# A graph layer that gathers some of its rows by picking columns: VectorE's 32 picks a run in three groups instead of two

## The chip, the cores and the metric

The kernel runs on one core of one Trainium2 chip. The metric is the time of one execution on the device in microseconds; lower is better. The core's engines are TensorE (PE in the profile, with its weight loads as PEld), VectorE (DVE), ScalarE (ACT), GpSimd (POOL) and SyncE (SP). Each has its own instruction queue, which runs in order. What a queue executes itself, such as loading registers or waiting, is shown as DVEq, ACTq, POOLq, SPq.

## The reference

A message-passing layer over a graph of N = 12,500 nodes with 128 features and E = 412,500 edges, sorted by their target node, with a residual connection and a layer norm.

```python
f0 = x0 @ W1_0e / sqrt(32);  f1 = einsum('nui,uw->nwi', x1, W1_1o) / sqrt(32)   # per node
e0, e1 = feat0[edge_src], feat1[edge_src]                 # a row of 128 gathered per edge
h = gelu(edge_scalar_attr @ W_mlp1 / sqrt(8));  h = gelu(h @ W_mlp2 / sqrt(64)) # per edge
w00, w01, w10, w11 = h @ Wp_00, h @ Wp_01, h @ Wp_10, h @ Wp_11
out0_a = w00 * e0 * ea0
out0_b = w11 * sum(e1 * ea1[:, None, :], -1) / sqrt(3)
out1_a = (w01 * e0)[:, :, None] * ea1[:, None, :]
out1_b = w10[:, :, None] * e1 * ea0[:, :, None]
n0, n1 = segment_sum(mid0, edge_dst), segment_sum(mid1, edge_dst)               # over edges
y = cos(pi/8) * self + sin(pi/8) * (n @ W2 / sqrt(64))    # scalar part and vector part
result = layernorm(x + y)
```

## The kernel before, in words

**Runs and groups.** The edges are cut into 806 runs `s` of 512, a run into four columns `q` of 128 edges. Four runs make a group `c` (CH = 4; k = s mod 4 is the place in the group). One loop over the runs issues everything, and the order in it is the order on the engines: PE, ACT, DVE and SP are scheduled by hand, so each queue executes its instructions as the loop writes them.

**Ahead of the loop.** The node rows are turned (`xT`, nodes along the free dimension, kept in on-chip memory for all 12,500 nodes) and multiplied by `wf` into the table of features. The first 18 runs ("raw" runs) gather rows of x and make their features themselves (`turn_rows`, `features`, L555 to L569); the later ones gather from the table.

**The rows of a run** land in a buffer `G` with four columns; 19 such buffers are in use (LEAD). A column is filled in one of four ways:
- by GpSimd's indirect DMA of 128 rows (`gather`, L210), which is the ordinary way;
- in every 14th run one column by 128 small DMAs on SyncE's queue (`aid`, L193 and L197);
- in every fourth run (18, 22, ...) column 2 by VectorE: it copies 128 columns of `xT`, one for each edge, into a tile `gt` (`pick`, L178). Then TensorE multiplies `gt` by `wf` (`picked_rows`, L186) and ScalarE copies the product into `G` (L187), two runs ahead of use;
- in the same manner column 1 in about every fifth run by ScalarE (L180).

The address of a picked column is a number from the input. So ahead of a group of picks, its engine's queue loads that many numbers from on-chip memory into registers (`pick_nodes`, L167, `TENSOR_LOAD`), and each copy reads its address from a register. VectorE picks 32 columns a run for one target; ScalarE picks 24 or 28 a run, 128 in five runs. Picks are spread over the runs ahead of their target. `COL_TURN` says in which run they begin and at which place k in a group their product stands: k = 0 for VectorE's picks, k = 1 for ScalarE's. So ScalarE's targets stand 4 or 8 runs apart.

**VectorE in a run.** `messages` makes the products of weights `w` (PSUM) and rows `G` in three instructions, 0 (L592, 128x256), 1 and 2 (L596, 128x384 each), into `M`. Between them stand the picks:

```python
messages(s, 0)
messages(s, 1)
pick_nodes(DVE, s, 0, 2)     # load 16 addresses
pick(DVE, P // 16)           # 8 copies
messages(s, 2)
pick_nodes(DVE, s, 1, 2)     # load 16 addresses
pick(DVE, P)                 # the 24 that are left
```

At k = 2 an addition of the last group's sums follows (`add`, L636); at k = 3 the selection for the next group (`select`: `oh` L577, then `own` L585). About every eighth group ends with a normalisation (`moments`, `normalise`), in which VectorE takes statistics (`bst`, L665) of what TensorE and ScalarE made of the sums (`y`, L656 and L661). Afterwards parts of the accumulator are cleared, one in a run (L406).

**TensorE in a run:** weights of coming runs (L550), sums of the run before (L621, L623, which need `M` and `own`), at k = 0 also the turning of edge attributes (L508), then `picked_rows` if one is due, then at k = 2 and 3 the two layers of the small network (`mlp1` L517, `mlp2` L532). ScalarE evaluates their gelu (L521, L537). The turning, the picked product and both layers take their PSUM tiles from one pool, "h", of two buffers.

Of the kernel before, what the change touches and what calls it, by code (L numbers as in the profile page):

```python
# [8 lines left out]
F32 = mybir.dt.float32  # L9
# [3 lines left out]
AF = mybir.ActivationFunctionType  # L13
OP = mybir.AluOpType
PE = mybir.EngineType.PE
ACT = mybir.EngineType.Activation
DVE = mybir.EngineType.DVE
# [4 lines left out]
P = 128  # L22
# [4 lines left out]
SB = P * Q  # L27
J = 8
CH = 4
# [18 lines left out]
AID_FROM = 36  # L48
AID_LEAD = 16
STEPS = 12  # L50
COLS = {DVE: 4, ACT: 5}
COL_Q = {DVE: Q - 2, ACT: Q - 3}
COL_TURN = {DVE: (8, 0), ACT: (16, 1)}
LNB = 2


# [1 line left out]
def gnn_kernel(ctx: ExitStack, tc: tile.TileContext, x, src, dst, ea4, ea8, w1_0, w1_1, wm1, wm2,  # L58
# [8 lines left out]
    nc = tc.nc  # L67
    N, F = x.shape
    E = src.shape[0]
    NS = -(-E // SB)  # L70
# [7 lines left out]
    raw_runs = min(RAW, NS)  # L78

    cst = ctx.enter_context(tc.tile_pool(name="cst", bufs=1))  # L80
    wk = ctx.enter_context(tc.tile_pool(name="wk", bufs=2))
# [3 lines left out]
    def sub(ap, offset, dims):  # L85
        return bass.AP(tensor=ap.tensor, offset=ap.offset + offset, ap=dims)


    x_at, _ = nc.bump_sbuf(4 * N)
    xT = nc.alloc_sbuf_tensor_at("xT", [P, N], F32, offset=x_at).ap()  # L90
    x_bytes = xT.bitcast(U8)
    x_bytes = bass.AP(tensor=x_bytes.tensor, offset=x_bytes.offset - x_at, ap=[[4 * N, P], [1, x_at + 4 * N]])
# [18 lines left out]
    G, GT, Y = {}, {}, {}  # L111
    aided = range(AID_FROM, NS - 1, AID)

    picked = {}
    for e, per in COLS.items():
        picked[e], (t, k) = [], COL_TURN[e]
        while True:
            at = t + per + 1
            at += (k - at) % CH
            if at + 2 >= NS - 1:  # L120
                break
            picked[e].append((t, at, at + 2))
            t += per
    pick_of = {(e, s): i for e, g in picked.items() for i, (_, _, s) in enumerate(g)}
    assert AID_FROM >= raw_runs and AID_LEAD < LEAD and P % ROWS == 0 and STEPS <= AID
    assert all(raw_runs <= g[0][2] and 0 < len(g) <= 2 * P for g in picked.values())
    assert 0 < len(aided) <= P

    aid_at = cst.tile([len(aided), P], I32)
    pick_rows = {}  # L130

    def aid_load():


        nc.sync.dma_start(aid_at, sub(src, AID_FROM * SB + (Q - 1) * P, [[AID * SB, len(aided)], [1, P]]))
        for e, g in picked.items():
            cycle = CH // math.gcd(CH, COLS[e])
            for h in range(0, len(g), P):
                part = g[h:h + P]
                rows = cst.tile([len(part), P], I32, name=f"pick{len(pick_rows)}")  # L140
                for i in range(min(cycle, len(part))):
                    n = len(part[i::cycle])
                    nc.sync.dma_start(rows[i::cycle], sub(src, part[i][2] * SB + COL_Q[e] * P,
                                                          [[cycle * COLS[e] * SB, n], [1, P]]))
                pick_tiles.append(rows)
                for i in range(len(part)):
                    pick_rows[e, h + i] = rows[i:i + 1]
# [7 lines left out]

    picking = {e: [] for e in picked}

    def pick_nodes(e, s, part=0, parts=1):

        per = COLS[e]  # L160
        i, t = divmod(s - COL_TURN[e][0], per)
        if not 0 <= i < len(picked[e]):
            return
        if t == 0 and part == 0:
            GT[e, i] = wk.tile([P, P], F32, name=f"gt{list(picked).index(e)}", bufs=3)
        r0, r1 = (n * (P // 4) // (per * parts) * 4 for n in (t * parts + part, t * parts + part + 1))
        _, r = nc.values_load_multi_w_load_instructions(  # L167
            pick_rows[e, i][:, r0:r1], engines=[e], min_val=x_at, max_val=x_at + 4 * (N - 1),
            skip_runtime_bounds_check_because="addresses of columns")
        for k in range(r1 - r0):  # L170
            at = r[k].with_bounds(guaranteed_mod_val=0, out_of_modulus=4)
            picking[e].append((GT[e, i][:, r0 + k:r0 + k + 1], x_bytes[:, bass.ds(at, 4)].bitcast(F32)))

    def pick(e, n):

        for to, col in picking[e][:n]:
            if e == DVE:
                nc.vector.tensor_copy(to, col)  # L178
            else:
                nc.scalar.activation(to, col, AF.Copy)  # L180
        del picking[e][:n]

    def picked_rows(e, i):

        pt = ps.tile([P, P], F32, name="h")
        nc.tensor.matmul(pt, GT.pop((e, i)), wf, start=True, stop=True)  # L186
        nc.scalar.activation(G[picked[e][i][2]][:, COL_Q[e], :], pt, AF.Copy)  # L187

    def aid(s, t):

# [397 lines left out]
    def messages(s, part):  # L588
        w, g = WP[s], G[s]
        if part == 0:  # L590
            M[s] = wk.tile([P, Q, 2, P], F32, name="M", bufs=3)
            nc.vector.tensor_tensor(M[s][:, :, :, :MUL], w[:, :, :2 * MUL].rearrange("p q (a u) -> p q a u", a=2),  # L592
                                    g[:, :, None, :MUL].to_broadcast([P, Q, 2, MUL]), op=OP.mult)
            return
        j = part - 1
        nc.vector.tensor_tensor(M[s][:, :, j, MUL:].rearrange("p q (i u) -> p q i u", i=3),  # L596
                                w[:, :, None, (2 + j) * MUL:(3 + j) * MUL].to_broadcast([P, Q, 3, MUL]),
                                g[:, :, MUL:].rearrange("p q (i u) -> p q i u", i=3), op=OP.mult)
# [221 lines left out]
    with tc.manual_schedule(engines={PE, ACT, DVE, SP}):  # L820
# [34 lines left out]
        if aided:  # L855
            aid_load()
# [9 lines left out]
        features(0)  # L866
        A["now"] = A["next"]
        clearing = []
        pick_nodes(ACT, 0)
        for s in range(NCH * CH + CH):  # L870
            c, k = divmod(s, CH)
            if s + LEAD - 1 < NS:
                gather(s + LEAD - 1)
            if k == 3 and c + EDGES_AHEAD < NCH:
                load_edges(c + EDGES_AHEAD)
            if s % P == P // 2 - 16 and (s // P + 1) * P < NS:
                load_raws(s // P + 1)
            if s % P == P // 2 and (s // P + 1) * P < NS:
                load_indices(s // P + 1)
            if s % ET == 8 and s - 8 + ET < NS:  # L880
                load_attributes(s // ET + 1)
            for t in range(P // ROWS):
                a = s + AID_LEAD - t * STEPS // (P // ROWS)
                if a in aided:
                    aid(a, t)
            end = c == NCH - 1
            if k % 2 == 0:
                pick(ACT, len(picking[ACT]) // 2)
            if k % 2 == 0 and s + 2 < NS:
                weights(s + 2, range(Q // 2))  # L890
            if k % 2 == 1 and s + 1 < NS:
                weights(s + 1, range(Q // 2, Q))
            if 0 < s <= NS:
                segments(s - 1)
            if k == 0 and c < NCH:
                places(c)
            if k == 0 and c + 2 < NCH:
                radial(c + 2)
            if s % ET == 21 and s - 21 + ET < NS:
                turn_attributes(s // ET + 1)  # L900
            for e in picked:
                if (e, s + 2) in pick_of:
                    picked_rows(e, pick_of[e, s + 2])
            if k > 1 and c + 2 < NCH:
                pick(ACT, P)
                (mlp1 if k == 2 else mlp2)(c + 2)
                if k == 3 and c + 3 == NCH:
                    nc.scalar.activation(spent, ones, AF.Sqrt)
            pick(ACT, P)
            pick_nodes(ACT, s + 1)  # L910
            if s + 1 < raw_runs:
                turn_rows(s + 1)
            if s < NS:
                messages(s, 0)
                messages(s, 1)
                pick_nodes(DVE, s, 0, 2)
                pick(DVE, P // 16)
                messages(s, 2)
                pick_nodes(DVE, s, 1, 2)
                pick(DVE, P)  # L920
            if s + 1 < raw_runs:
                features(s + 1)
            if k == (1 if end else 2) and 0 < c <= NCH:
                add(c - 1)
            if k == (1 if end else 3) and 0 < c <= NCH:
                norm(due.get(c - 1, []), last=c == NCH)
                clearing += [(c, a) for a in range(4)] if c - 1 in due and c < NCH else []
            elif clearing:
                clear_sums(clearing.pop(0)[1])
            if k == 3 and c + 1 < NCH:  # L930
                select(c + 1)
            if s == 1:
                addresses()
                find_first()
                new_sums()
                clearing = [(0, a) for a in range(4)]
            if s == NS - 8:
                count_odd()
# [31 lines left out]
```

## Time and profile before

| | |
|---|---|
| median of 3 runs | 3773.7 us |
| lowest, highest | 3766.81, 3779.11 us |
| profiled execution | 3772.84 us |
| its span, first to last instruction | 3771.0 us |
| granted TensorE clock, mean | 0.914 |
| table gathers by GpSimd (L210) | 2743 |
| picked columns, VectorE (L178) | 25216, in 788 runs |
| picked columns, ScalarE (L180) | 19968 |

Engine times in the profile are busy times of one execution. "Idle before, releaser" is the time that the engine stood still right ahead of such an instruction, and what ended it; "issue" means that the engine waited for nothing that the profile shows, only for its queue to hand it the instruction. The timeline's rows give the start in us from the start of the span, the duration in us, then engine, line and operation, and a count where several like ones are merged. Durations of neighbours overlap a little, so what an instruction takes of the engine's time is read from the starts.

### The profile page before, as it was taken

What the parts mean: (1) busy time and instruction counts of PE and PEld (TensorE: products, weight loads), DVE (VectorE), ACT (ScalarE), POOL (GpSimd) and SP (SyncE); (2) the same over time, 40 slices, a digit from 0 to 9 for tenths busy, and PEclk for the clock granted to TensorE, in tenths of its full rate; (3) what the DMA queues carried; (4) which work ended last, traced back from release to release, by engine and by line L of the source; (5) the groups of instructions that cost most, each with busy time, mean ns of one, the idle gap of its engine ahead of it and who ended that gap; (6) DMA issues with size and microseconds to landing.
All of it is one profiled execution on the core that took longest, in us unless ns stands there. A gap on an engine that the chain in (4) does not pass through costs nothing.

```text
span 3771.0 us, 139554 instructions
## 1 busy us (share of the span) xinstructions
PE 3274.6 (87%) x28566; PEld 2859.2 (76%) x28566; DVE 3106.1 (82%) x28801; ACT 2594.3 (69%) x21604; POOL 2682.6 (71%) x2821
## 2 busy tenths in 40 slices
PE   5888898888898889888889898898898888888998
PEld 4677777777777778777778777777787777777877
DVE  3488888888888888888888888888888888888886
ACT  2367677777767767767777677776776677767774
POOL 7567777777777777777777777777777777767770
PEclk8999898998988999899998899999899999989889
DMA  8222222323222223222223222222322222222220
GB/s 203 47 51 67 61 56 65 64 57 70 61 58 64 63 57 68 64 55 62 62 63 67 61 63 61 61 62 61 68 62 59 59 64 61 60 63 63 58 61 15
DMA packets 579462, 240.07 MB, mean 64 GB/s; under 512 B 483793, under 2 KB 528744, under 8 KB 578616
## 3 DMA queue, kind: packets, MB, share of 16 engines
q0 software_dynamic: 90080, 184.66, 19.1%
q1 hardware_dynamic: 467766, 39.95, 8.7%
q10 hardware_dynamic: 20770, 6.47, 0.7%
q8 instruction: 252, 4.13, 0.5%
q14 instruction: 594, 4.87, 0.4%
HBM read 218.04 MB, written 12.80 MB: 61 GB/s over the span
## 4 chain that ended last, share of the span: by engine, by line
DVE 51%; issue 12%; PE 10%; SPq 9%; DVEq 6%; ACT 5%; DMA 4%; POOL 2%; ACTq 0%; POOLq 0%
DVE gt L178 29%; DVE M L596 14%; SPq L197 7%; DVEq L167 6%; DVE M L592 3%; ACT gt L180 3%; PE sums L621 2%; POOL G L210 2%; PE sums L623 2%; SPq L193 2%; PE h L656 2%; DMA G<-table,idx 1%; DVE acc L636 1%; PE w L550 1%; PE h L517 1%
## 5 line engine op out<-in xcount | busy, mean ns | idle before, releaser
L210 POOL DMA_INDIRECT G<-table,idx x2743 | 2613.7, 953 | 981.2 <-issue 758.4
L180 ACT ACTIVATE gt<-xT 128x1 f32 x19968 | 1953.4, 189 | 255.9 <-issue 254.2
L178 DVE COPY gt<-xT 128x1 f32 x25216 | 1680.1, 144 | 374.2 <-issue 362.4
L623 PE MATMUL sums<-own,M 128*128 128x96 f32 x6446 | 1342.7, 292 | 63.2 <-DVE M L596 62.7
L621 PE MATMUL sums<-own,M 128*128 128x96 f32 x6446 | 1374.7, 297 | 25.0 <-DVE M L596 24.8
L621 PEld LDWEIGHTS sums<-own,M 128*128 128x128 f32 x6446 | 1063.9, 205 | 115.4 <-DVE M L596 31.1
L623 PEld LDWEIGHTS sums<-own,M 128*128 128x128 f32 x6446 | 1061.4, 207 | 84.1 <-DVE M L596 83.2
L550 PE MATMUL w<-wpb,h 64*128 64x128 f32 x6448 | 726.8, 310 | 255.8 <-DVE M L596 254.9
L550 PEld LDWEIGHTS w<-wpb,h 64*128 64x128 f32 x6448 | 540.4, 200 | 426.8 <-DVE M L596 305.8
L596 DVE TENSOR_TENSOR M<-w,G 128x384 f32<-128x384 f32 x1576 | 861.2, 547 | 0.1
L521 ACT ACTIVATE h<-h 128x512 f32<-128x512 f32 x404 | 216.2, 585 | 225.0 <-PE h L517 219.2
L592 DVE TENSOR_TENSOR M<-w,G 128x256 f32<-128x256 f32 x788 | 321.6, 408 | 3.6 <-ACT G L187 2.0
L517 PE MATMUL h<-eT,w1b 64*128 64x128 f32 x3232 | 299.9, 339 | 4.2 <-ACT eT L510 4.2
L517 PEld LDWEIGHTS h<-eT,w1b 64*128 64x128 f32 x3232 | 255.8, 237 | 29.6 <-issue 12.5
L187 ACT ACTIVATE G<-h 128x128 f32<-128x128 f32 x353 | 96.2, 272 | 261.1 <-PE h L186 218.1
L532 PE MATMUL h<-h,w2b 64*64 64x256 f32 x3232 | 236.5, 392 | 7.4 <-ACT h L521 6.3
L537 ACT ACTIVATE h<-h 128x512 f32<-128x512 f32 x404 | 213.6, 578 | 25.1 <-PE h L532 20.0
L532 PEld LDWEIGHTS h<-h,w2b 64*64 64x64 f32 x3232 | 111.1, 133 | 60.5 <-ACT h L521 16.1
L186 PE MATMUL h<-wf,gt 128*128 128x128 f32 x706 | 145.7, 289 | 4.1 <-ACT eT L510 4.1
L585 DVE TENSOR_TENSOR own<-oh,e 128x512 f32<-128x512 f32 x202 | 139.7, 692 | 7.1
L665 DVE BATCH_NORM_STATS2 bst<-h 128x6 f32<-128x128 f32 x98 | 26.9, 274 | 131.2 <-ACT y L661 123.0
L510 ACT ACTIVATE eT<-h 128x128 f32<-128x128 f32 x202 | 53.8, 267 | 111.1 <-PE h L508 105.2
(112 smaller groups left out, 1364.5 us busy)
## 6 DMA issues: line engine op xcount, KB each, us to landing
G<-table SPq DMA_DIRECT2D x7040, 0.5 KB
G<-table,idx POOLq DMA_INDIRECT x2743
e<-in_edge_attr SPq DMA_DIRECT2D x201, 64.0 KB
xt<-in_x SPq DMA_DIRECT2D x24, 256.0 KB
table<-ft ACTq DMA_DIRECT2D x24, 256.0 KB
xt<-in_edge_attr SPq DMA_DIRECT2D x24, 256.0 KB
out<-y SPq DMA_DIRECT2D x24, 256.0 KB
xt<-in_dst SPq DMA_DIRECT2D x5, 256.0 KB
```

Of the source, the lines that this page charges most:

```text
L167: _, r = nc.values_load_multi_w_load_instructions(pick_rows[e, i][:, r0:r1], engines=[e], min_val=x_at, max_val=x_at + 4 * (N - 1), skip_r ...
L178: nc.vector.tensor_copy(to, col)
L180: nc.scalar.activation(to, col, AF.Copy)
L197: nc.sync.dma_start(G[s][r0 + k:r0 + k + 1, Q - 1, :].bitcast(U8), table_bytes[bass.ds(r[k], P * 4)].rearrange("(a k) -> a k", a=1))
L210: nc.gpsimd.indirect_dma_start(out=G[s][:, q, :], out_offset=None, in_=x if s < raw_runs else table, in_offset=bass.IndirectOffsetOnAxis(a ...
L517: nc.tensor.matmul(p1[h][:, j // 2, j % 2, :], w1b[rows, j, :], eT[c][rows, :], start=True, stop=True)
L532: nc.tensor.matmul(p2[r][k * HID:(k + 1) * HID, h * n:(h + 1) * n], w2b[rows, :], H1[c][h][rows, k * n:(k + 1) * n], start=True, stop=True)
L550: nc.tensor.matmul(WP[i][:, q, :], H2[c][q % 2][rows, k, q // 2, :], wpb[rows, :], start=True, stop=True)
L592: nc.vector.tensor_tensor(M[s][:, :, :, :MUL], w[:, :, :2 * MUL].rearrange("p q (a u) -> p q a u", a=2), g[:, :, None, :MUL].to_broadcast( ...
L596: nc.vector.tensor_tensor(M[s][:, :, j, MUL:].rearrange("p q (i u) -> p q i u", i=3), w[:, :, None, (2 + j) * MUL:(3 + j) * MUL].to_broadc ...
L621: nc.tensor.matmul(flat[:, bass.ds(at, 4 * FIRST_HALF)].bitcast(F32), M[s][:, q, 0, :], own[:, 3 * WIDE:], start=False, stop=False)
L623: nc.tensor.matmul(sb[:, 1:, bass.ds(at, 4 * WIDE)].bitcast(F32), M[s][:, q, 1, :], own[:, :3 * WIDE].rearrange("p (a j) -> p a j", a=3), ...
```

## The change

VectorE's picks of a run stand in three groups of 8, 12 and 12, one behind each product of messages, each with a load of just that many addresses ahead of it. Before, there were two loads of 16, one behind the second and one behind the third product, with 8 and 24 copies. The number of picks is the same.

The groups are now listed in `SLOTS`, and a picked tile is multiplied two runs behind the run that completes it, at whatever place in the group that is. VectorE's picks begin in run 11 instead of 8; its targets (18, 22, ...) stay, and its product stays at k = 0. ScalarE's groups of a run become 24, 28, 24, 28, 24 (before 24, 24, 28, 24, 28), its targets 24, 29, 34, ... (before 27, 31, 35, 39, 47, ...), and its product falls on all four places k in turn. GpSimd leaves out the gathers of those columns instead.

```diff
-COLS = {DVE: 4, ACT: 5}
+SLOTS = {DVE: [(8, 12, 12)], ACT: [(24,), (28,), (24,), (28,), (24,)]}
-COL_TURN = {DVE: (8, 0), ACT: (16, 1)}
+COL_FROM = {DVE: 11, ACT: 16}
...
+    slot_at = {}
+    for e, cycle in SLOTS.items():
+        slot_at[e], n = {}, 0
+        for s in range(COL_FROM[e], NS):
+            for slot, k in enumerate(cycle[(s - COL_FROM[e]) % len(cycle)]):
+                slot_at[e][s, slot] = (n, n + k)
+                n += k
+
     picked = {}
-    for e, per in COLS.items():
-        picked[e], (t, k) = [], COL_TURN[e]
+    for e in SLOTS:
+        picked[e] = []
         while True:
-            at = t + per + 1
-            at += (k - at) % CH
+            last = P * (len(picked[e]) + 1)
+            at = next((s for (s, _), (_, z) in slot_at[e].items() if z >= last), NS) + 2
             if at + 2 >= NS - 1:
                 break
-            picked[e].append((t, at, at + 2))
-            t += per
+            picked[e].append(at + 2)
...
-    def pick_nodes(e, s, part=0, parts=1):
+    def pick_nodes(e, s, slot):
 
-        per = COLS[e]
-        i, t = divmod(s - COL_TURN[e][0], per)
-        if not 0 <= i < len(picked[e]):
-            return
-        if t == 0 and part == 0:
-            GT[e, i] = wk.tile([P, P], F32, name=f"gt{list(picked).index(e)}", bufs=3)
-        r0, r1 = (n * (P // 4) // (per * parts) * 4 for n in (t * parts + part, t * parts + part + 1))
-        _, r = nc.values_load_multi_w_load_instructions(
+        a, z = slot_at[e].get((s, slot), (0, 0))
+        z = min(z, P * len(picked[e]))
+        while a < z:
+            i, r0 = divmod(a, P)
+            r1 = min(P, r0 + z - a)
+            if r0 == 0:
+                GT[e, i] = wk.tile([P, P], F32, name=f"gt{list(picked).index(e)}", bufs=3)
+            _, r = nc.values_load_multi_w_load_instructions(
...
-                messages(s, 0)
-                messages(s, 1)
-                pick_nodes(DVE, s, 0, 2)
-                pick(DVE, P // 16)
-                messages(s, 2)
-                pick_nodes(DVE, s, 1, 2)
-                pick(DVE, P)
+                for part in range(3):
+                    messages(s, part)
+                    pick_nodes(DVE, s, part)
+                    pick(DVE, P)
```

More of the change, by code (lines that the diff above doesn't have):

```diff
@@ L112, in gnn_kernel @@
     aided = range(AID_FROM, NS - 1, AID)
+    slot_at = {}
[5 more added lines that the diff above has]
+                n += k
     picked = {}
-    for e, per in COLS.items():
-        picked[e], (t, k) = [], COL_TURN[e]
+    for e in SLOTS:
+        picked[e] = []
         while True:
-            at = t + per + 1
-            at += (k - at) % CH
+            last = P * (len(picked[e]) + 1)
+            at = next((s for (s, _), (_, z) in slot_at[e].items() if z >= last), NS) + 2
             if at + 2 >= NS - 1:
                 break
-            picked[e].append((t, at, at + 2))
-            t += per
-    pick_of = {(e, s): i for e, g in picked.items() for i, (_, _, s) in enumerate(g)}
+            picked[e].append(at + 2)
+    pick_of = {(e, s): i for e, g in picked.items() for i, s in enumerate(g)}
     assert AID_FROM >= raw_runs and AID_LEAD < LEAD and P % ROWS == 0 and STEPS <= AID
-    assert all(raw_runs <= g[0][2] and 0 < len(g) <= 2 * P for g in picked.values())
+    assert all(raw_runs <= g[0] and 0 < len(g) <= 3 * P for g in picked.values())
     assert 0 < len(aided) <= P
@@ L136, in aid_load @@
         for e, g in picked.items():
-            cycle = CH // math.gcd(CH, COLS[e])
+            n = sum(sum(run) for run in SLOTS[e])
+            cycle, ahead = n // math.gcd(n, P), P // math.gcd(n, P) * len(SLOTS[e])
+            assert all(z - a == ahead for a, z in zip(g, g[cycle:]))
             for h in range(0, len(g), P):
@@ L141, in aid_load @@
                 for i in range(min(cycle, len(part))):
-                    n = len(part[i::cycle])
-                    nc.sync.dma_start(rows[i::cycle], sub(src, part[i][2] * SB + COL_Q[e] * P,
-                                                          [[cycle * COLS[e] * SB, n], [1, P]]))
+                    k = len(part[i::cycle])
+                    nc.sync.dma_start(rows[i::cycle], sub(src, part[i] * SB + COL_Q[e] * P,
+                                                          [[ahead * SB, k], [1, P]]))
                 pick_tiles.append(rows)
@@ L156, in gnn_kernel @@
     picking = {e: [] for e in picked}
-    def pick_nodes(e, s, part=0, parts=1):
-        per = COLS[e]
-        i, t = divmod(s - COL_TURN[e][0], per)
-        if not 0 <= i < len(picked[e]):
-            return
-        if t == 0 and part == 0:
-            GT[e, i] = wk.tile([P, P], F32, name=f"gt{list(picked).index(e)}", bufs=3)
-        r0, r1 = (n * (P // 4) // (per * parts) * 4 for n in (t * parts + part, t * parts + part + 1))
[L167 to L172, printed above, removed]
+    def pick_nodes(e, s, slot):
[7 more added lines that the diff above has]
+            _, r = nc.values_load_multi_w_load_instructions(
+                pick_rows[e, i][:, r0:r1], engines=[e], min_val=x_at, max_val=x_at + 4 * (N - 1),
+                skip_runtime_bounds_check_because="addresses of columns")
+            for k in range(r1 - r0):
+                at = r[k].with_bounds(guaranteed_mod_val=0, out_of_modulus=4)
+                picking[e].append((GT[e, i][:, r0 + k:r0 + k + 1], x_bytes[:, bass.ds(at, 4)].bitcast(F32)))
+            a += r1 - r0
     def pick(e, n):
@@ L186, in picked_rows @@
         nc.tensor.matmul(pt, GT.pop((e, i)), wf, start=True, stop=True)
-        nc.scalar.activation(G[picked[e][i][2]][:, COL_Q[e], :], pt, AF.Copy)
+        nc.scalar.activation(G[picked[e][i]][:, COL_Q[e], :], pt, AF.Copy)
     def aid(s, t):
@@ L868, in gnn_kernel @@
         clearing = []
-        pick_nodes(ACT, 0)
+        pick_nodes(ACT, 0, 0)
         for s in range(NCH * CH + CH):
@@ L909, in gnn_kernel @@
             pick(ACT, P)
-            pick_nodes(ACT, s + 1)
+            pick_nodes(ACT, s + 1, 0)
             if s + 1 < raw_runs:
```

## Prediction

> **What bounds the kernel now.** I read the page first, for the busy shares and the costliest groups, then the list of waits, then VectorE's timeline through one group of four runs, then the loads of registers.
>
> ```profile
> PE 3274.6 (87%) x28566; PEld 2859.2 (76%) x28566; DVE 3106.1 (82%) x28801; ACT 2594.3 (69%) x21604; POOL 2682.6 (71%) x2821
> L180 ACT ACTIVATE gt<-xT 128x1 f32 x19968 | 1953.4, 189 | 255.9 <-issue 254.2
> L178 DVE COPY gt<-xT 128x1 f32 x25216 | 1680.1, 144 | 374.2 <-issue 362.4
> ```
>
> Four engines are between 69% and 87% busy, so the shares do not name the bound. TensorE has the largest, but its matmuls overlap. What decides is who waits for whom (microseconds in total, times, longest):
>
> ```profile
> DVE gt L178 <- issue: 362.4, 907, 1.3
> PE w L550 <- DVE M L596: 254.9, 241, 2.1
> POOL G L210 <- DVE M L596: 134.8, 129, 9.9
> DVE bst L665 <- ACT y L661: 123.0, 23, 8.9
> DVE M L592 <- ACT ft L569: 57.3, 18, 14.3
> ```
>
> TensorE and GpSimd wait for VectorE's messages (`M`). VectorE waits for others in two places only: in the first 18 runs (57.3 us for `ft`) and at a normalisation (123.0 us for `y`). Its largest idle time, 362.4 us, has the reason "issue": nothing it depends on was late. So VectorE sets the pace, and what it loses to "issue" is on the path. One group of runs, VectorE alone:
>
> ```profile
> 2012.38 0.41 DVE L592 TENSOR_TENSOR M<-w,G 128x256 f32<-128x256 f32 x1
> 2012.71 0.55 DVE L596 TENSOR_TENSOR M<-w,G 128x384 f32<-128x384 f32 x1
> 2013.20 0.58 DVE L178 COPY gt<-xT 128x1 f32 x8
> 2013.69 0.55 DVE L596 TENSOR_TENSOR M<-w,G 128x384 f32<-128x384 f32 x1
> 2014.68 1.55 DVE L178 COPY gt<-xT 128x1 f32 x24 [0.44 <-issue]
> 2016.14 0.42 DVE L592 TENSOR_TENSOR M<-w,G 128x256 f32<-128x256 f32 x1
> ...
> 2020.37 0.42 DVE L592 TENSOR_TENSOR M<-w,G 128x256 f32<-128x256 f32 x1
> ...
> 2024.04 0.28 DVE L577 TENSOR_TENSOR oh<-iota,rel 128x128 f32<-128x128 f32 x1
> 2024.35 0.69 DVE L585 TENSOR_TENSOR own<-oh,e 128x512 f32<-128x512 f32 x1
> 2024.96 0.42 DVE L592 TENSOR_TENSOR M<-w,G 128x256 f32<-128x256 f32 x1
> ```
>
> A plain run takes 2016.14 - 2012.38 = 3.76 us: 0.33 for the first product, 0.49 for the second, 0.49 for 8 columns, 0.55 for the third product, an idle 0.44, and 1.46 for 24 columns, 0.061 each. The idle stands right behind the second load of column addresses, which the timeline does not show because the queue executes it and not the engine. The view of line 167 (min/median/max ns, first and last start) shows it, over the whole run and in three narrow windows around this run:
>
> ```profile
> L167 DVEq TENSOR_LOAD <-pick x1576: 1093/1122/1740, 149.6 to 3716.9; - x197
> L167 DVEq TENSOR_LOAD <-pick x1: 1098/1098/1098, 2012.0 to 2012.0; - x1
> L167 DVEq TENSOR_LOAD <-pick x1: 1122/1122/1122, 2013.5 to 2013.5; - x1
> L167 DVEq TENSOR_LOAD <-pick x1: 1103/1103/1103, 2015.8 to 2015.8; - x1
> L592 DVEq EVENT_SEMAPHORE  x1833: 21/50/4408, 209.1 to 3750.8; - x184
> ```
>
> The queue loads from 2012.0 to 2013.1, issues 8 columns and a product in the 0.4 us to 2013.5 (about 0.04 each), loads to 2014.6, issues 24 columns, two waits of 0.05 and two products, and loads again at 2015.8. It never rests, its waits take no longer than the 50 ns of the median, and its cycle, 2015.8 - 2012.0, is the run's period. In a plain run the queue is the pacer, not the engine, which has 3.32 us of work in 3.76.
>
> **The change, part by part.** *Three loads for two.* The columns stay 32 a run. The queue issues the same 32 copies, 3 products and waits, but loads 8 + 12 + 12 addresses instead of 16 + 16. If a load costs a fixed part a and the rest by its addresses, the queue's cycle grows by exactly a. No row shows a load of 8 or 12 on VectorE; the nearest are its loads of 4 (line 631) and of 16 above, and ScalarE's of 28 and 24:
>
> ```profile
> L631 DVEq TENSOR_LOAD <-first_at x51: 342/348/766, 135.8 to 3751.0; - x51
> L631 DVEq TENSOR_LOAD <-first_at x16: 345/570/576, 1314.3 to 2393.3; - x16
> L167 ACTq TENSOR_LOAD <-pick x1: 1737/1737/1737, 2002.1 to 2002.1; - x1
> L167 ACTq TENSOR_LOAD <-pick x1: 1536/1536/1536, 2005.9 to 2005.9; - x1
> ```
>
> From 348 and 1122: (1122 - 348) / 12 = 64.5 ns an address and a = 348 - 258 = 90 ns. So 8 cost 0.61, 12 cost 0.86, and a run 2.33 for 2.24. Lower end: strictly proportional, a = 0. Upper end: from VectorE's 16 to ScalarE's 24, (1536 - 1122) / 8 = 52 ns each, a = 0.29; the slow loads of 4 (570 in the second window) would even give 0.39. I take 0.09, because both of its rows are VectorE's own and lie on either side of 8 and 12.
>
> Of the 788 runs with picks (25216 / 32), three of each four are paced by the queue (two plain ones, and the one with the addition): 591 x 0.09 = +53 us.
>
> *The run before a selection.* In the fourth, `own` (L585) needs `oh` (L577), and `oh` needs all columns executed, so the engine's end counts and not the queue's. Behind the last load 24 columns are left at 0.061 now, of which 12 would instead be issued earlier at 0.04: 12 x 0.021 = 0.25 us less, plus a. 197 x (0.09 - 0.25) = -32 us.
>
> *Where the idle goes.* Counted from the first load: loaded at 0.61, eight columns and a product issued by 0.97, load to 1.83, twelve and a product by 2.35, load to 3.21, twelve by 3.69. Eight columns and a product keep the engine busy 1.0 us and twelve 1.2, each against a load plus issuing. So the one idle of 0.44 becomes three of 0.15 to 0.25, some 0.53 together. The smaller load hides no better, since less work is queued in front of it.
>
> *Messages later in the run.* The third product ends 1.9 us ahead of the run's end now (0.44 + 1.46), then about 0.9. TensorE's sums and weights get it a microsecond later, once, and VectorE does not wait for them. Only at a normalisation does a chain come back to VectorE: messages, sums, `y`, then `bst`. There up to 0.9 us is added, 23 times: 0 to +21, I take +18, because VectorE idles there already (123.0 us), so nothing covers it.
>
> *Picks three runs later.* VectorE starts at run 11 instead of 8 and ends at 798 instead of 795. The three early runs are in the stretch that waits for `ft`, so nothing is won there; the three late ones get 32 columns each, 32 x 0.061 + 0.44 = 2.4 us, next to waits of VectorE that are there already. 0 to +7; I take +5.
>
> *ScalarE.* Its groups are the same size in another order. The product of its picked rows (L186, L187) now falls into any of the four runs of a group rather than the second, so it can stand ahead of the two layers, which use the same two PSUM buffers. VectorE does not wait for those layers except at the normalisation, and one in four or five of the 23 meets it: five times a ScalarE group of 28 copies at 1953.4 / 19968 = 0.098 each, 2.7 us, is the most, and as much could be won where the product leaves the second run: -13 to +13, I take +4. Fewer or earlier gathers gain nothing, as GpSimd already waits for VectorE. Buffers of `gt` are held for less time, and no row shows a wait for one.
>
> Sum: +53 - 32 + 18 + 5 + 4 = +48 us. The profiled execution took 3772.8 us (span 3771.0), 0.9 below the median of the three runs, so the sum goes on the median: 3773.7 + 48 = 3822 us.
>
> [...] Row: the engine idles 0.44 us behind a product while a load of 1.12 runs, with 24 ready columns behind it. [...]
>
> **Rivals.** *A load's fixed part is nil* (the other side): loads cost 70 ns an address and nothing more. Then the queue-paced runs stay, the selection runs win 197 x 0.25 = 49 us, and with +18 + 5 + 4 it ends at 3752; if none of these three costs come, at 3725. It decides below a = 0.25 / 4 = 0.06, where a group of four breaks even, without the three costs. For it speaks that a load of 4 is measured in two sizes, so the line through it is uncertain; against it, that 348 ns for 4 is more than a quarter of 1122.
>
> *A dearer load*: a = 0.29. 591 x 0.29 - 197 x (0.25 - 0.29) = 171 + 8, and 27: 3980. The 570 ns rows and ScalarE's pair speak for it; against it, two thirds of the 51 loads of 4 are near 348.
>
> *Loads do not pace*: something else absorbs 0.09 us a run, as columns being issued early, and the time stays at 3774. The 0.44 us in each plain run speaks against it.
>
> **How the numbers follow.** Forecast 0.62, nil 0.16, dearer 0.13, no pacing 0.09. A measurement of this kernel tells about 0.3%, 11 us, from no change. The forecast holds for a from 0.05 to 0.2, which is 3790 to 3909 by the same sum; 0.59 of its 0.62 is slower, 0.02 faster, 0.01 within. The dearer load is slower throughout, nil is faster in 0.15 and within in 0.01, no pacing is within in 0.08 and faster in 0.01. Hence faster 0.15 + 0.02 + 0.01 = 0.18, within 0.10, slower 0.59 + 0.13 = 0.72. The range runs from 3740, inside the nil case, to 3935, part of the way to the dearer one; about 0.05 lies below it and 0.1 above.
>
> **What would show it.** Right: 2364 loads on VectorE in two sizes near 0.61 and 0.86; plain runs of 3.85 us with three idles; the run before a selection, 4.59 now (2020.37 to 2024.96), about 4.43; idle to "issue" near 390 us; `bst` waiting some 140. Wrong: loads of 8 below 0.56 or above 0.7, a plain run below 3.76, or VectorE waiting for TensorE's `w` or for ScalarE's `G`, which it does not do now.

## The result and the profile after

| | before | after |
|---|---|---|
| median | 3774.73 us (4 runs) | 3827.24 us (4 runs) |
| lowest, highest | 3766.81, 3779.11 | 3823.22, 3829.21 |
| ratio to before | | 1.0136, 95% interval 1.012 to 1.0153 |
| span of the profiled execution | 3771.0 us | 3821.1 us |

The change makes the kernel 1.4% slower; 3822 us was forecast. The page's busy times and its two costliest groups on ScalarE and VectorE, for the changed kernel (lines have moved by about ten: L188 are the picked columns, L176 their loads, L602 and L606 the products, L675 the statistics):

```profile
PE 3349.3 (88%) x28568; PEld 2931.5 (77%) x28568; DVE 3186.1 (83%) x28801; ACT 2612.3 (68%) x21733; POOL 2675.8 (70%) x2820
L190 ACT ACTIVATE gt<-xT 128x1 f32 x20096 | 1971.2, 189 | 322.9 <-issue 321.0
L188 DVE COPY gt<-xT 128x1 f32 x25216 | 1758.0, 144 | 298.4 <-issue 202.3
```

Its waits:

```profile
DVE gt L188 <- issue: 202.3, 914, 0.5
PE w L560 <- DVE M L606: 205.6, 176, 2.2
POOL G L220 <- DVE M L606: 167.2, 132, 12.1
DVE bst L675 <- ACT y L671: 147.9, 23, 11.1
DVE M L602 <- ACT ft L579: 64.4, 18, 11.8
```

VectorE is still what the others wait for. Its listed idle to "issue" fell from 362.4 to 202.3 us, and yet it takes longer. Two things hide that. Its busy time rose by 80 us with the same 28,801 instructions. Most of that is no new work: an instruction overlaps the next one (the 384 wide products last 0.55 us and what follows at once starts after 0.46 to 0.49; the copies last 0.144 and start 0.061 apart), and where nothing follows at once, its whole end counts as busy. Summed in the trace, 60 of the 80 us are such ends of the three products, behind each of which the engine now stands still, and 19 are ends of copies. And its idle as a whole (span less busy) fell only from 664.9 to 635.0, since many of the new idles are too small to be listed. TensorE's busy time rose too, by 75 us for two matmuls more, at a granted clock of 0.894 for 0.914. One plain run on VectorE in the timeline:

```profile
2033.54 0.41 DVE L602 TENSOR_TENSOR M<-w,G 128x256 f32<-128x256 f32 x1
2034.07 0.58 DVE L188 COPY gt<-xT 128x1 f32 x8
2034.56 0.55 DVE L606 TENSOR_TENSOR M<-w,G 128x384 f32<-128x384 f32 x1
2035.27 0.82 DVE L188 COPY gt<-xT 128x1 f32 x12 [0.16 <-issue]
2036.01 0.55 DVE L606 TENSOR_TENSOR M<-w,G 128x384 f32<-128x384 f32 x1
2036.61 0.82 DVE L188 COPY gt<-xT 128x1 f32 x12
2037.34 0.41 DVE L602 TENSOR_TENSOR M<-w,G 128x256 f32<-128x256 f32 x1
```

The view by line of VectorE's queue (min/median/max ns, first and last start), over the whole execution, has its loads and waits:

```profile
L176 DVEq TENSOR_LOAD <-pick x2364: 591/848/1341, 164.5 to 3772.4; - x197
L641 DVEq TENSOR_LOAD <-first_at x51: 340/344/760, 133.7 to 3800.6; - x51
...
L602 DVEq EVENT_SEMAPHORE  x1934: 21/50/5133, 208.2 to 3800.4; - x194
```

The run takes 3.80 us, and the engine stands still behind each product: 2034.07 is 0.20 later than the 0.33 of the first product would have it, and by the 0.49 of the other two the second group of columns starts 0.22 late and the third 0.11. Over all runs the loads of 8 have a median of 0.607 us and those of 12 of 0.866.

Where the 50 us of the two profiled executions went, summed in the trace from the start of one run's first product to the next:

| us | before | after | difference |
|---|---|---|---|
| up to run 18 | 209.7 | 208.6 | -1 |
| 755 runs without a normalisation | 3220.1 | 3235.4 | +15 |
| 23 runs with one | 290.7 | 318.5 | +28 |
| from run 796 to the end | 50.6 | 58.6 | +8 |

### The profile page after: what moved, and what is told of

It is laid out like the page before. It is cut to its first block, busy times and chain, and to the rows that moved or that the text cites. A ratio compares the mean times of both kernels' runs of the same rounds, so it can differ in the third digit from the quotient of the medians.

```text
span 3821.1 us, 140526 instructions
## 1 busy us (share of the span) xinstructions
PE 3349.3 (88%) x28568; PEld 2931.5 (77%) x28568; DVE 3186.1 (83%) x28801; ACT 2612.3 (68%) x21733; POOL 2675.8 (70%) x2820
## 4 chain that ended last, share of the span: by engine, by line
DVE 51%; PE 14%; issue 10%; DVEq 7%; SPq 7%; ACT 5%; DMA 4%; POOL 2%; ACTq 0%; POOLq 0%
DVE gt L188 30%; DVE M L606 14%; DVEq L176 6%; SPq L207 5%; DVE M L602 4%; PE sums L631 3%; PE sums L633 3%; ACT gt L190 3%; PE h L666 2%; DMA G<-table,idx 2%; PE w L560 2%; POOL G L220 2%; PE h L527 2%; SPq L203 1%; DMA xt<-in_x 1%
## 5 line engine op out<-in xcount | busy, mean ns | idle before, releaser
L188 DVE COPY gt<-xT 128x1 f32 x25216 | 1758.0, 144 | 298.4 <-issue 202.3
L631 PE MATMUL sums<-own,M 128*128 128x96 f32 x6446 | 1396.1, 301 | 32.4 <-DVE M L606 32.2
L633 PE MATMUL sums<-own,M 128*128 128x96 f32 x6446 | 1361.6, 296 | 50.1 <-DVE M L606 49.5
L631 PEld LDWEIGHTS sums<-own,M 128*128 128x128 f32 x6446 | 1088.6, 209 | 123.8 <-DVE M L606 38.9
L633 PEld LDWEIGHTS sums<-own,M 128*128 128x128 f32 x6446 | 1082.2, 211 | 65.9 <-DVE M L606 65.3
L606 DVE TENSOR_TENSOR M<-w,G 128x384 f32<-128x384 f32 x1576 | 861.6, 547 | 0.3
L560 PEld LDWEIGHTS w<-wpb,h 64*128 64x128 f32 x6448 | 552.0, 206 | 368.3 <-DVE M L606 245.3
L527 PE MATMUL h<-eT,w1b 64*128 64x128 f32 x3232 | 327.1, 348 | 9.1 <-ACT G L197 5.2
L602 DVE TENSOR_TENSOR M<-w,G 128x256 f32<-128x256 f32 x788 | 321.9, 408 | 10.3 <-ACT G L197 4.6
L527 PEld LDWEIGHTS h<-eT,w1b 64*128 64x128 f32 x3232 | 278.0, 244 | 39.7 <-issue 15.3
L542 PE MATMUL h<-h,w2b 64*64 64x256 f32 x3232 | 250.6, 394 | 5.0 <-ACT h L531 4.7
L196 PE MATMUL h<-wf,gt 128*128 128x128 f32 x708 | 155.0, 303 | 28.3 <-ACT eT L520 25.3
L675 DVE BATCH_NORM_STATS2 bst<-h 128x6 f32<-128x128 f32 x98 | 26.9, 274 | 157.7 <-ACT y L671 147.9
L196 PEld LDWEIGHTS h<-wf,gt 128*128 128x128 f32 x708 | 116.4, 206 | 36.4 <-ACT eT L520 33.3
```

The costliest lines, as they stand in the source:

```text
L527: nc.tensor.matmul(p1[h][:, j // 2, j % 2, :], w1b[rows, j, :], eT[c][rows, :], start=True, stop=True)
L542: nc.tensor.matmul(p2[r][k * HID:(k + 1) * HID, h * n:(h + 1) * n], w2b[rows, :], H1[c][h][rows, k * n:(k + 1) * n], start=True, stop=True)
L560: nc.tensor.matmul(WP[i][:, q, :], H2[c][q % 2][rows, k, q // 2, :], wpb[rows, :], start=True, stop=True)
L631: nc.tensor.matmul(flat[:, bass.ds(at, 4 * FIRST_HALF)].bitcast(F32), M[s][:, q, 0, :], own[:, 3 * WIDE:], start=False, stop=False)
L633: nc.tensor.matmul(sb[:, 1:, bass.ds(at, 4 * WIDE)].bitcast(F32), M[s][:, q, 1, :], own[:, :3 * WIDE].rearrange("p (a j) -> p a j", a=3), ...
```

## The experiments

The theory at this point: VectorE's queue sets the pace; a third load costs its fixed part and a restart behind it; shorter rows of copies give some of that back. The rival: ScalarE's new places for its product are what costs, or the load count does not matter.

The three series ran on three chips. On the chip of the second series the kernel before takes 3779.53 us, its usual time. On those of the first and the third it takes 5509.34 and 5565.53 us. So the second series carries the argument, and what the other two showed comes at the end of this section.

**The three groups alone.** ScalarE's groups, targets and places are those of before.

```diff
-SLOTS = {DVE: [(8, 12, 12)], ACT: [(24,), (28,), (24,), (28,), (24,)]}
+SLOTS = {DVE: [(8, 12, 12)], ACT: [(24,), (24,), (28,), (24,), (28,)]}
...
+            if e == ACT:
+                at += (1 - at) % CH
```

> The same kernel as e1_dve_only, wanted beside a kernel before that takes its usual time of about 3774 us (in the first series it took 5509 us). VectorE's three groups alone. Theory (VectorE's queue sets the pace, and the third load is the cost): nearly all of the difference, 1.011 to 1.015 times the kernel before, 3815 to 3830 us. Rival (ScalarE's new places for its product): under half of it, 3775 to 3800.

Measured: 3802.36 us, 1.0054 times before (1.0033 to 1.0075). The intervals of this and of the whole change do not touch, so the theory missed: the groups are not nearly all of the difference. By the ratio they are 0.4 of it, 20 us, as the rival had it (its 3800 is missed by 2 us); by the profiled spans (3804.3 - 3771.0, from two series) they are 33 us. The rest of the change costs between 17 us (3821.1 - 3804.3) and 31 us (0.0082 of the median), more than the +4 of the prediction. Its waits:

```profile
DVE gt L192 <- issue: 196.0, 876, 0.6
DVE bst L679 <- ACT y L675: 145.7, 23, 10.2
```

The longer wait at a normalisation (145.7, against 123.0 before) is here already, so it comes from the groups and not from ScalarE's places; the mechanism that the rival gave does not hold. What ScalarE's places add is spread in this pair of traces: 5 us in normal runs, 4 at normalisations, 5 behind run 796, 2 at the start. One part of it can be counted: VectorE's queue executes more instructions that wait on semaphores ahead of the products.

```profile
L606 DVEq EVENT_SEMAPHORE  x1833: 21/50/4316, 205.8 to 3784.0; - x184
```

That is 1833, as in the kernel before, and 1934 with the whole change; one follows another at 0.098 us in the trace, so 101 more are at most 10 us where the queue paces.

**Two loads of 16, each with its own 16 copies**, the rest as changed.

```diff
-SLOTS = {DVE: [(8, 12, 12)], ...
+SLOTS = {DVE: [(0, 16, 16)], ...
```

> The same kernel as e3_16_16: two loads of 16, each followed at once by its own 16 copies. Theory (0.03 us a copy, 0.09 of restart behind a load, 24 copies in a row fill the queue): plain runs of 3.68 us, near 3705 us, 3690 to 3725. Rival, the prediction's own model (0.04 a copy, queue never full): plain runs of 3.76 us, near 3758.

Measured: 3735.48 us, 0.9875 times before (0.9859 to 0.9892). It beats both kernels, with the same number of loads as before and all else as changed.

```profile
L176 DVEq TENSOR_LOAD <-pick x1576: 1093/1124/2105, 162.3 to 3686.6; - x197
DVE gt L188 <- issue: 224.5, 870, 1.3
DVE bst L675 <- ACT y L671: 156.2, 22, 11.3
```

The loads are as many and as long as before. Plain runs take 3.73 us from one first load to the next (median), where they took 3.85 before: 0.12 less. The theory forecast 3.68 against the 3.76 of the run shown, 0.08 less, and the prediction's model no change. The 755 normal runs take 3140.1 us, 80 less than before. The time as a whole missed the 3690 to 3725 and lies between the two forecasts, since the normalisations cost 40 us more than before rather than 16, and ScalarE's places are in it. So the plain runs decide for the theory, not the time.

**Five loads for three.** Each load of 12 is made as one of 4 and one of 8, in a row.

```diff
-            _, r = nc.values_load_multi_w_load_instructions(pick_rows[e, i][:, r0:r1], ...
+            cut = [r0, r0 + (r1 - r0) // 2 // 4 * 4, r1] if e == DVE and r1 - r0 > 8 else [r0, r1]
+            r = []
+            for c0, c1 in zip(cut, cut[1:]):
+                r += nc.values_load_multi_w_load_instructions(pick_rows[e, i][:, c0:c1], ...)[1]
```

> The same kernel as e4_five_loads: each load of 12 made as a load of 4 and one of 8. Theory: loads of 2.51 us a run for 2.34, +0.17 in 788 runs, near 3960 us, 3940 to 3975; if the two loads in a row also pay the 0.09 of restart between them, 3960 to 4100. Rival (loads are no longer the pacer): 3825 to 3850.

Measured: 4079.14 us, 1.0789 times before (1.0771 to 1.0807): 252 us above the changed kernel, for two more loads a run and nothing else. The range of 3940 to 3975 is missed; the one with a restart between two loads in a row, 3960 to 4100, holds, and the rival is out.

```profile
DVE gt L191 <- issue: 509.1, 1700, 0.7
```

and its loads, by line:

```profile
L179 DVEq TENSOR_LOAD <-pick x3940: 340/598/844, 161.0 to 4028.8; - x197
```

The trace closes the account. Loads of 4 take 0.349 and of 8 0.605 where one of 12 took 0.866, so 0.088 is the fixed part, and the second of the two begins 0.073 behind the end of the first. 2 x (0.088 + 0.073) x 788 = 254 us. The queue is the pacer, and a load more costs 0.16 us of it.

**Statistics two runs later**, from the copy of `y` in on-chip memory instead of PSUM. The changed kernel otherwise.

```diff
-            nc.vector.bn_stats(st[:k, t, :], pt[:k, t, :])
+            nc.vector.bn_stats(st[:k, t, :], Y["y"][:k, j, t, :])
...
+            if k == 1 and stats:
+                finish()                 # statistics and normalise() of the group before
```

> The changed kernel, with VectorE's statistics of a normalisation taken two runs later and from the copy y in on-chip memory instead of PSUM, and the scaling and store of the output behind them. The same work is done. Theory (the wait of bst for y, 148 us in the changed kernel and 123 before, is on the path, and the later third product lengthened it by 25): the wait goes nearly to zero but for the last group, 3690 to 3715 us. Rival (that time is slack for TensorE, which then becomes the late one, and VectorE waits for w instead): 3770 to 3827.

Measured: 3783.63 us, 1.0016 times before (1.0001 to 1.0031), 44 us below the changed kernel. The wait of 147.9 us is gone; this took its place:

```profile
DVE acc L416 <- ACT acc L419: 83.9, 22, 6.8
DVE rs L689 <- ACT rs L688: 25.8, 13, 3.6
```

The next run's clearing of an accumulator now waits for ScalarE's move of the sums, which stands behind the same chain. The time is the one that the rival gave, but not for its reason: VectorE waits 1.5 us for `w`. So the normalisation's wait is on the path, but taking away the first thing that waits for it wins only what the next one does not need.

**The first and the third series.** The first series had the groups alone, the other parts alone (two loads of 16 with 8 and 24 copies), the two loads of 16 with 16 copies each, and the five loads:

> VectorE's three groups of 8, 12 and 12 alone; ScalarE's groups, targets and places are those of the kernel before. Theory (VectorE's queue sets the pace, and the third load is the cost): nearly all of the difference is here, 3815 to 3830 us. Rival (the picked product of ScalarE, now ahead of the layers of the small network, delays TensorE and ScalarE, above all at the normalisations): under half of it, 3775 to 3800, and the wait of the statistics for y back near 123 us.

> Everything of the change but the three groups: ScalarE's new groups and targets and the start at run 11 stay, VectorE loads 16 and 16 with 8 and 24 copies as before. Theory: 3770 to 3790 us, plain runs of 3.76 to 3.79 us, one idle of 0.44 us each. Rival (ScalarE's places): 3795 to 3815, with a wait for y near 148 us.

> Two loads of 16, each followed at once by its own 16 copies (behind the second and the third product), the rest as changed. Theory as read from the two traces (a copy issues in 0.03 us, a load costs 0.09 of restart behind it, and 24 copies in a row fill VectorE's queue so that it waits 0.13): cycle of the queue 2 x 1.122 + 2 x 0.09 + 32 x 0.03 + 0.2 of waits + 0.09 = 3.68 in a plain run, 0.24 less in a run before a selection, some 0.7 more at each of 23 normalisations: near 3705 us, 3690 to 3725. Rival, the prediction's own model (0.04 a copy, queue never full): plain runs unchanged, 8 x 0.021 less before a selection: near 3758.

> As changed, but each load of 12 is made as a load of 4 and one of 8 in a row; the copies and their order stay. So two more loads a run, of the same addresses. Theory (each load's fixed part of 0.09 us is on the path): loads 0.607 + 2 x (0.346 + 0.607) = 2.51 a run for 2.34, +0.17 in 788 runs, so 3825 + 137 = 3960 us, 3940 to 3975. Rival (the queue is not the pacer in the changed kernel, its third load and the later third product only shift work): 3825 to 3850.

Measured against 5509.34 us: 5575.24 (1.0117, 1.0089 to 1.0145), 5543.51 (1.0073, 1.0052 to 1.0094), 5556.02 (1.0097, 1.0077 to 1.0117) and 5586.7 (1.0142, 1.0115 to 1.0168). Two loads of 16 with 16 copies each, which won 1.25% on the chip of the second series, lose 1% here, and five loads lose 1.4% instead of 7.9%. Something else paces. In the third series, where the kernel before is as slow, were the other parts alone once more, the 16 and 16 with ScalarE's old places, the same with statistics and clearing delayed, and the changed kernel with both delays:

> The same kernel as e2_two_loads, wanted beside a kernel before of its usual time: the change without the three groups. By the series of f1_dve_only (groups alone: 1.0054) against the whole change (1.0136), the rest of the change should cost 15 to 30 us: 3790 to 3810. If the two parts do not add (the groups are dear only with ScalarE's new places): 3770 to 3785.

> Two loads of 16, each followed by its own 16 copies, with ScalarE's groups and targets as before the change. Theory: the kernel f3_16_16 less what ScalarE's places cost, 15 to 30 us: 3703 to 3722, so 0.980 to 0.985 times the kernel before. If the parts do not add: 3735.

> As g1_16_16_old, and the normalisation's statistics taken two runs later from y in on-chip memory, and the clearing of the next accumulator begun two runs later than that, so that it no longer waits for ScalarE's move of the sums (83.9 us in f5_defer). Theory (both waits are on the path): 3710 less some 130 us: near 3590, not under what GpSimd needs, 2742 gathers at 0.95 + 0.30 us and 180 us around them, about 3600 to 3620. Rival (TensorE's chain at a normalisation is late for the weights w too): 3640 to 3690.

> The changed kernel with both of these delays. f5_defer took the statistics off the chain and gained 44 us of 148, because the clearing took over 84 us of the wait. Theory: with the clearing off it too, 3784 - 84 = 3700, 3690 to 3715. Rival (TensorE is the late one next): 3730 to 3784.

Measured against 5565.53 us: 5583.09 (1.0032, 1.0019 to 1.0046), 5573.29 (1.0014, 1.0 to 1.0029), 5474.19 (0.9834, 0.9807 to 0.9861) and 5556.84 (0.9981, 0.9965 to 0.9998). Most of the expectations were for a kernel before of the usual time and cannot be judged here. The 16 and 16 with both delays beats the same without them (5474.19 for 5573.29), and the rest of the change alone is slower in both series, by 0.7% and by 0.3%. That agrees in sign with the difference of the second series. But none of these numbers says what a part costs where the queue paces. What ScalarE's places cost alone, and what the two delays and the 16 and 16 together bring, was not measured on a chip of the usual time and stays open.

## Why the prediction was right

**The bound** was read rightly. In the changed kernel VectorE waits for others at the same places, and two more loads a run cost 252 us in full, so the rival by which loads do not pace is out. In none of the 1628 loads of the kernel before does VectorE's queue start another instruction of its own.

**A load's fixed part**, the disputed number, was taken as 0.09 from loads of 4 and of 16. The loads of 8 and 12 came out at 0.607 and 0.866 (0.61 and 0.86 forecast). Both rivals on it, nil and 0.29, are out.

**The queue-paced runs**, +53, came to 50, but not as the sum had them. Summed in the trace from one first load to the next, which is how the prediction counts the queue's cycle, the two plain kinds of run cost 10 and 15 us and the run with the addition 25. Plain runs went from 3.85 to 3.88 and from 3.85 to 3.91 us in the median, not up by 0.09 each. The step that failed is "It never rests". The prediction took 0.04 us to issue a copy by dividing a stretch among its instructions. The gaps between loads in three kernels separate it: 8 copies and a product take 0.360, 12 and one 0.481, 16 and one 0.602. A copy issues in 0.030, and a load leaves 0.073 of restart behind it, as the two loads in a row show. In the kernel before, behind 24 copies, the stretch up to the next first load is 1.19 where 16 with the same waits and products take 0.83 (two loads of 16); eight more at 0.030 would make 1.07. So 0.12 is left for which 0.030 a copy does not account; the author's estimate is that the queue waited there for the engine, which needs 0.061 a copy. The change adds 0.09 of fixed part and 0.07 of restart and takes away the 0.12, which leaves 0.04, about what the plain runs show. Why the run with the addition lost more, 0.13 in the mean, stays open.

In the traces of plain runs, the queue comes to its first wait 0.459 us behind the end of its last load where 12 copies stand between (the changed kernel, median) and 0.939 where 24 do (the kernel before): 0.480 for twelve copies more, where 0.030 each would make 0.36. At that wait ten of the 24 have not begun (270 of 388 runs); behind 12 copies it is six (289 of 388), behind 16 it is eight. The gaps behind 8, 12 and 16 copies grow by 0.121 from one to the next, so of these rows of copies only that of 24 shows the 0.12. That the queue waits for room there was not shown.

**The run before a selection**, -32, came to -30 by the same count, and is 0.19 us shorter at the median (4.79 to 4.61), 0.16 forecast. From product to product, as the prediction gives it under what would show it (4.59 to 4.43), it is not shorter: 4.58 before and 4.64 after at the median. By that count the saving, 32 us, stands in the run behind it, and the other three cost 18, 20 and 8. So the normal runs together cost 21 us from load to load, as 53 - 32 had it, and 15 from product to product.

**The normalisations** cost 28 us from product to product (22 from load to load), against 18; with the groups alone it is 23. The mechanism is the one named, the third product that comes later in the run. In the 23 runs with a normalisation it starts 1.38 us behind the first product before and 2.35 with the groups alone (means), and the statistics start 7.61 and 7.65 us behind it. The bound of 0.9 us each was a little low: 1.0 us in that kernel, 1.2 in the whole change. With two loads of 16 the statistics start 8.8 us behind the third product, so there something else is late as well. TensorE's granted clock is lower in the profiles of the changed kernel (0.894) and of the second series (0.901 with the groups alone, 0.898 with two loads of 16, 0.868 with five loads, 0.9 with the later statistics) than in that of the kernel before (0.914); whether that lengthens this chain was not tested.

**The late picks and ScalarE.** Behind run 796 the groups alone cost 3 us and the whole change 8, against 5. ScalarE's places were put at +4 with the argument that VectorE does not wait for the layers. Here a term was mis-sized: they cost 17 to 31 us. The prediction counted the engines' waits and left out that each wait is also an instruction in VectorE's queue. That explains at most 10 us; the rest was not settled.

**What was expected in the profile.** The loads, the three idles of a plain run (0.53 us together in the one shown, counted from the starts; some 0.53 forecast), its length (3.80 in that run, about 3.9 at the median, for 3.85) and `bst` (147.9 for some 140) came. The run before a selection did not, by the prediction's own count. Nor did the idle to "issue": 202 us instead of 390. The page's 298.4 us for all idle ahead of the copies has the pieces under 0.15 us, which are not listed, and the ends of products that count as busy hide 60 us more.

So the total was 5 us off. By stretch, 15 + 28 + 8 - 1 = 50 us came where 21 + 18 + 5 + 4 = 48 were forecast. By part it is less good: the groups alone cost 20 us by the ratio or 33 by the spans where 44 were forecast, and ScalarE's places 17 to 31 where 4 were. The bound, the load's fixed part and the direction were understood; that the total came this close is luck, since the two errors cancel.

## What to carry to other kernels

Where an engine copies columns whose addresses come from registers, look at what its queue does and not only at the engine: count each load of registers (0.607 us here for 8 addresses, 0.866 for 12), each wait (0.098 from one to the next) and each issued copy (0.030), and compare that sum with the engine's work. Splitting a load to place its work better cost a fixed part and a restart each time, 0.16 us here, which pays only if the idle that it fills is larger. The better edit was to leave the number of loads and shorten the row of copies behind the last one from 24 to 16: 0.9875 times the kernel before, where the change has 1.0136.

## What the runs showed of the hardware

In the third series, where the kernel before takes 5565.53 us, several engines stand still together for stretches. The timeline of the 16 and 16 kernel with ScalarE's old places shows three engines that each issue one instruction and stop, again and again in common steps of about 0.7 us:

```profile
3001.06 0.15 DVE L192 COPY gt<-xT 128x1 f32 x1 [0.55 <-issue]
3001.79 0.20 ACT L194 ACTIVATE gt<-xT 128x1 f32 x1 [1.15 <-issue]
3001.79 0.15 DVE L192 COPY gt<-xT 128x1 f32 x1 [0.58 <-issue]
3001.81 0.24 PE L637 MATMUL sums<-own,M 128*128 128x96 f32 x1 [0.89 <-issue]
...
3002.51 0.20 ACT L194 ACTIVATE gt<-xT 128x1 f32 x1 [0.52 <-issue]
3002.53 0.15 DVE L192 COPY gt<-xT 128x1 f32 x1 [0.58 <-issue]
...
3003.91 0.29 ACT L194 ACTIVATE gt<-xT 128x1 f32 x2 [1.20 <-issue]
3003.91 0.29 DVE L591 TENSOR_TENSOR oh<-iota,rel 128x128 f32<-128x128 f32 x1 [1.24 <-issue]
```

From the start of one copy on VectorE to that of the next in the row more than 0.45 us pass 1696 times in this profile, and never in that of the kernel before at 3771 us. GpSimd, in the same timeline, starts its gathers 1.24 to 1.25 us apart meanwhile (2999.52, 3000.77, 3002.01). The granted TensorE clock was 0.759 (0.914 in the kernel before's profile), and VectorE's idle to "issue" 1388.0 us. In the kernel with the groups alone, in the first series, the loads of addresses take the same 0.607 and 0.866 us. What holds the engines was not found, nor whether it belongs to the chip or to its state at the time.
